# Two-layer masked attention on one core: the reciprocals of layer 1's softmax sums taken later, and its last group counted once

## The chip, the cores and the metric

The kernel runs on one core of a Trainium2 chip. The metric is the device time of one execution in microseconds (us); lower is better. The core has a matmul engine (TensorE, PE), three engines for elementwise work (VectorE, DVE; ScalarE, ACT; GpSimd, POOL) and SyncE (SP), whose queue issues most transfers. Each engine works through its own queue in order and waits on semaphores. PSUM is the memory that PE writes, SBUF the working memory of all engines.

## What is computed

Sixteen graphs of 1,024 nodes with 256 features pass through two layers. Each layer is: layer norm and ReLU, attention over the neighbours that the adjacency allows, an output projection, and a sum with the layer's input. Layer 0 has 4 heads of 64, layer 1 has 8 heads of 32. Cut to what matters:

```python
h = jnp.maximum(_layernorm(x, axis=-1), 0.0)
q, k, v = heads(h @ Wq.T + bq), heads(h @ Wk.T + bk), heads(h @ Wv.T + bv)
scores = jnp.einsum('bhnd,bhmd->bhnm', q, k) / math.sqrt(D)
w = jax.nn.softmax(jnp.where(adjacency == 0, -jnp.inf, scores), axis=-1)
out = jnp.einsum('bhnm,bhmd->bhnd', w, v)
x = x + out.transpose(0, 2, 1, 3).reshape(b, n, e) @ Wo.T + bo
```

Layer 0 has no biases of q, k and v. Everything is float32.

## The kernel before

**Groups and steps.** For one graph and one layer, a group is half of the rows (`qh`, 512 queries) and half of the features (`g`, 128 partitions: two heads in layer 0, four in layer 1). A layer has four groups, in the order (qh 0, g 0), (0, 1), (1, 0), (1, 1); the last has `gr.last` set. A group is worked in steps: 8 in layer 1 (one tile of 128 keys for four heads), 4 in layer 0 (two tiles for two heads). One step is: four score matmuls into PSUM (`scores`, L400); on DVE the mask by a minimum (L416) and on ACT the exponential (L421), each in two halves, which give the tile `p` (`exponentials`); two steps later (`LEAD = 2`) the matmuls of `p` with the values into `po` (`weigh`, L433). The softmax is not shifted by a maximum. It divides at the end, so each group also needs the sums of its `p`.

**The stream.** All steps stand in one list: layer 0 of the next graph, layer 1 of this graph, and so on, so a period is 16 steps of layer 0 and 32 of layer 1. `Stream.run` (L479) records them one by one. Other work is put into a table of due work by `later(i, f)`: at step i, after the masks and exponentials. In an odd step `add_tiles` of layer 0 is recorded before what is due. In even steps with a large piece (`LARGE`: projections and `end_half`) the weighing is left to the next step. What is recorded later stands later in its engine's queue. Each engine follows its queue strictly.

**Sums of layer 1.** For every pair of steps POOL adds the odd tile to the even one (L534). An ordinary group chains its four even tiles by three accumulating transfers (`accumulate`, L520, from POOL's queue, 1 MB each): the first tile into the second at j = 3, the second into the third at j = 7, the third into the fourth three steps after that. Then the fourth is counted once, by matmuls with ones into `pz` (`count`, L301), 8 steps after j = 7 is weighed. The last group of a layer is `brief`: only the first transfer is made, and the second, third and fourth tile are counted one after the other into the same `pz`, all in one step. The last graph's groups (`pairs`, and `hurry` for the very last) count every pair.

**From sums to rows.** `end_group` (L558) sets the steps for what follows, relative to the step i in which the group's last step is weighed:
- `spread`: ACT copies `pz` to `s` (L320), and SP spreads one row per head over the partitions of `sums` (L333, four small transfers);
- `invert`: DVE takes the reciprocal (L341), SP writes it to DRAM (`vd`, L343) and reads it back broadcast (`inv`, L346, four transfers);
- `normalize`: POOL multiplies the group's half of `cat` by `inv` (L352);
- `end_half`, after the second group of a half: the output projection on PE (L381), the sum with the rows on DVE (L386) and, in layer 1, the store from SP (L388).

`inp.test`, seven steps after a layer's last group is weighed, lets DVE check that the sums lie in a range (L247). If they do not, a slower program runs afterwards; in the runs here it does not.

**Beside that.** For a later graph the adjacency is loaded in eight pieces from POOL's queue (L128), each is transposed by a transfer from SP's queue (`flip`, L134) and turned into a mask by ACT (`put`, L143). There is one buffer for a loaded piece, so the next load waits until the transpose is through. `open_x` loads the rows of a later graph (L115) into a buffer that a store has to release, and `half_inputs` and `norms` set the steps of the next layer's projections.

**Positions.** In the following a position is the place of a step in its period, counted from the first step of layer 0 (0 to 15), with layer 1 at 16 to 47; `a` in the code is position 0 and `c` position 16. The groups of layer 1 are weighed to their end at positions 25, 33, 41 and, for the last, 1 of the next period.

Of the kernel before, what the change touches and what calls it, by code (L numbers as in the profile page):

```python
# [82 lines left out]
def fast_program(ctx, tc, a, w, loads, chk):  # L83
# [5 lines left out]
    B, N, E = x.shape  # L89
# [29 lines left out]
    class Mask:  # L119
        def __init__(self, b):  # L120
            self.b, self.src, self.flipped, self.m = b, {}, {}, {}
# [150 lines left out]
    class Group:  # L272


        def __init__(self, inp, mask, qh, g, half):
            self.inp, self.mask, self.qh, self.g, self.half = inp, mask, qh, g, half
            self.layer = inp.layer
            self.D = E // HEADS[self.layer]
            self.per = P // self.D
            self.scale = 1.0 / math.sqrt(self.D)  # L280
            self.n = f"{inp.n}_{qh}_{g}"
            self.n_f = self.per * 512 // P
            self.last = qh == QH - 1 and g == 1

            self.hurry = False

            self.brief, self.pairs = self.last, False

        def steps(self):
            n_j = NT if self.layer else NT // 2  # L290
# [168 lines left out]
    class Stream:  # L459
# [12 lines left out]
        def later(self, i, f, *args):  # L472
            self.due.setdefault(i, []).append((f, args))
# [48 lines left out]
        def count_steps(self, i, st):  # L522


            gr, j = st.gr, st.j
            if gr.hurry and j >= NT - 2:
                if st.last:
                    self.counted(i, gr)
                gr.count(st.p, False, st.last)
            elif j % 2:  # L530
                one = self.steps[i - LEAD - 1].p
                if not (gr.brief or gr.pairs) and j == 7:
                    self.accumulate(gr.two, gr.one)
                nc.gpsimd.tensor_add(one, one, st.p)  # L534
                if gr.pairs:
                    self.later(i + 2, gr.count, one, j == 1, st.last)
                elif j == 1:
                    gr.one = one
                elif j == 3:
                    self.accumulate(one, gr.one)  # L540
                    gr.one = one
                    if gr.brief:
                        self.later(i + 8, gr.count, one, True, False)
                elif gr.brief:
                    self.later(i + (6 if j == 5 else 4), gr.count, one, False, st.last)
                elif j == 5:
                    gr.two = one
                else:
                    self.later(i + 3, self.accumulate, one, gr.two)
                    self.later(i + 8, gr.count, one, True, True)  # L550

        def counted(self, i, gr):

# [4 lines left out]
        def end_group(self, i, gr):  # L558

            if gr.hurry:  # L560
                for f in (gr.spread, gr.finish, gr.inp.test):
                    self.later(i, f)
                return

            if gr.layer == 0:
                self.later(i + 4, gr.count_added)
                at = 4, 6, 8, 11
            else:
                at = (8, 10, 15, 17)
                if gr.pairs:  # L570
                    at = 2, 5, 7, 9
                elif gr.brief:
                    at = 4, 7, 9, 11
            for k, f in zip(at, (gr.spread, gr.invert, gr.normalize)):
                self.later(i + k, f)
            if gr.last:

                k = 7 if gr.layer or gr.inp.b == 0 else 37
                self.later(i + k if gr.inp.b + gr.layer < B - 1 else len(self.steps) + 2, gr.inp.test)
            if gr.g == 1:  # L580
                self.later(i + at[3], gr.end_half)
# [8 lines left out]
    mask, inp = masks[0], inputs[0][0]  # L590
# [74 lines left out]
    later = stream.later  # L665

    def norms(inp, half, *at):

        for i, f in zip(at, (inp.stats, inp.stats, inp.norm, inp.norm)):
            later(i, f, half, (0, 1) if i in (at[0], at[2]) else (2, 3))  # L670
        later(at[3] + 1, inp.add_bias, half)

    def half_inputs(inp, half, *at):

        for i, f in zip(at, (inp.turn, inp.k, inp.q, inp.values)):
            later(i, f, half)
# [5 lines left out]
    for t in range(NT):  # L682
        i = 6 + 2 * t
# [8 lines left out]
    for b in range(B - 1):  # L692
        mine, a, c = inputs[1][b], first[b + 1], second[b]
        if b == 0:

            norms(mine, 0, a + 5, a + 6, a + 8, a + 9)
            half_inputs(mine, 0, a + 11, a + 12, a + 14, a + 14)
            norms(mine, 1, a + 13, a + 14, a + 15, c)
            half_inputs(mine, 1, c + 1, c + 3, c + 6, c + 4)
        else:  # L700
            norms(mine, 0, a - 20, a - 19, a - 16, a - 15)
            half_inputs(mine, 0, a - 13, a, a + 4, a + 8)
            norms(mine, 1, a - 14, a - 10, a - 8, a - 6)
            half_inputs(mine, 1, a - 1, c, c + 6, c + 2)
        for i, u in zip((0, 2, 4, 6, 8, 10, 12, 13), range(NT)):
            later(a + i, masks[b].second, u)
        if b + 2 < B:
            other, mask = inputs[0][b + 2], masks[b + 2]
            later(a + 3, open_x, b + 2, 0)
            later(a + 13, open_x, b + 2, 1)  # L710
            if b == 0:
                norms(other, 0, a + 14, a + 15, c + 2, c + 3)
                half_inputs(other, 0, c + 5, c + 8, c + 16, c + 18)
                norms(other, 1, c + 3, c + 4, c + 6, c + 7)
                half_inputs(other, 1, c + 11, c + 22, c + 26, c + 30)
            else:
                norms(other, 0, a + 10, a + 12, a + 13, a + 15)
                half_inputs(other, 0, c + 1, c + 8, c + 16, c + 18)
                norms(other, 1, c, c + 4, c + 5, c + 6)
                half_inputs(other, 1, c + 9, c + 22, c + 26, c + 30)  # L720
            for i, t in zip((7, 12, 17, 22, 33, 37, 41, 45), range(NT)):
                later(a + i - 5 + (t > 4), mask.load, t)
                later(a + i - 2, mask.flip, t)
                later(a + i, mask.put, t)
        else:
            last, e = inputs[1][b + 1], c + 32
            norms(last, 0, c + 5, c + 6, c + 8, c + 9)
            half_inputs(last, 0, c + 11, c + 14, c + 16, c + 20)
            norms(last, 1, c + 13, c + 14, c + 16, c + 17)
            half_inputs(last, 1, c + 19, c + 24, e + 6, e + 4)  # L730
            for u in range(NT):
                later(c + 8 + 2 * u, masks[b + 1].second, u)
# [158 lines left out]
def kernel(  # L891
# [28 lines left out]
    with ExitStack() as fast, tc.manual_schedule():  # L920
        fast_program(fast, tc, a, w, loads, chk)
# [61 lines left out]
```

## Time and profile before

| | |
|---|---|
| median of 3 runs | 3360.76 us (3353.34 to 3380.53) |
| the profiled execution | 3366.5 us |
| its span, first to last instruction | 3364.7 us |
| granted PE clock | 0.985 |
| accumulating transfers p<-p (L520) | 150, 1024 KB each, median 8.4 us from issue to landing |
| transposes of the adjacency (L134) | 124, 3.0 / 3.3 / 12.8 us to landing (least, median, most) |
| matmuls of the count (L301) | 1,112 records, 172.7 us busy |
| ACT's mask (L143) | 140.6 us busy, 28.1 us idle before it, waiting for transposes |
| POOL's normalizing multiply (L352) | 127, mean 1332 ns |
| median to landing: sums / vd of layer 1 / inv | 1.8 / 2.5 / 2.6 to 2.9 us |

The profile is one execution. Each engine's busy time is the union of its instructions; PE's matmuls are pipelined and their ends are modelled. A matmul in the program leaves two records. In a row of the timeline the first number is the start from the beginning of the span, the second the duration of the merged instructions; the square bracket at the end holds how long the engine was idle before it and what ended that. In the chain of waits each piece is what the end of the kernel hung on at that time.

### The profile page before, as it was taken

The page shows a single profiled execution, that of the slowest core. Times are in us where ns is not written, and L with a number is a line of the kernel's source. Part 1 is how long each engine was busy: PE and PEld are TensorE (multiplying, and loading weights), DVE is VectorE, ACT ScalarE, POOL GpSimd, SP SyncE. Part 2 cuts the span into 40 slices and gives each one's busy share as a digit, 9 for nine tenths or more (in the row PEclk, how much of TensorE's full clock was granted, in tenths as well). Part 3 has the DMA queues.
Part 4 walks back from the last instruction along what each step waited for, and adds up shares of the span by engine and source line. Part 5 has one row for each costly group of instructions (what it writes and reads, how often), then busy time and mean ns, then how long its engine had stood idle before and what let it go on. Part 6 is the DMA issues. An engine that isn't in the chain of part 4 may idle for free.

```text
span 3364.7 us, 44402 instructions
## 1 busy us (share of the span) xinstructions
PE 3267.3 (97%) x16990; PEld 1277.7 (38%) x16990; DVE 2518.0 (75%) x2760; ACT 2181.5 (65%) x2402; POOL 2347.4 (70%) x1244
## 2 busy tenths in 40 slices
PE   8999999999999999999999999999999999999898
PEld 3343333333433333343333433343343333433333
DVE  5776877768767787776877768777687777778876
ACT  6567576665756757667575665757667576674565
POOL 4578586775857758677585776857668586785776
PEclk9999999999999999999999999999999999999899
DMA  7348265472644826447273472736638365380431
GB/s 141 67 76 146 62 120 101 86 145 58 125 92 85 145 64 126 92 88 139 63 140 78 94 144 56 144 77 106 128 64 149 71 109 112 76 154 26 86 79 31
DMA packets 309453, 331.74 MB, mean 99 GB/s; under 512 B 189552, under 2 KB 257392, under 8 KB 290032
## 3 DMA queue, kind: packets, MB, share of 16 engines
q0 software_dynamic: 73824, 224.42, 37.1%
q1 hardware_dynamic: 235408, 104.41, 13.8%
q8 instruction: 135, 2.21, 0.3%
q14 instruction: 86, 0.70, 0.1%
HBM read 119.54 MB, written 17.56 MB: 41 GB/s over the span
## 4 chain that ended last, share of the span: by engine, by line
PE 77%; DMA 7%; ACT 5%; DVE 4%; POOL 3%; issue 2%; SPq 2%; DVEq 0%; ACTq 0%; POOLq 0%
PE ps L400 26%; PE po L433 23%; PE pq L225 11%; PE py L381 7%; PE pv L262 6%; PE pz L301 4%; DVE p L416 3%; DMA sums<-s 3%; DMA p<-p 3%; POOL p L534 3%; ACT p L421 2%; SPq L333 1%; DMA adjT<-adj 1%; ACT mask L143 1%; PE ph L208 1%
## 5 line engine op out<-in xcount | busy, mean ns | idle before, releaser
L421 ACT ACTIVATE p<-p 128x1024 f32<-128x1024 f32 x1536 | 1617.8, 1057 | 938.1 <-DVE p L416 892.4
L416 DVE SCALAR_TENSOR_TENSOR p<-mask,ps 128x1024 f32<-128x1024 fp8e4 x1536 | 1792.0, 1214 | 564.7 <-PE ps L400 547.8
L534 POOL TENSOR_TENSOR p<-p,p 128x2048 f32<-128x2048 f32 x255 | 1190.7, 4672 | 267.0 <-PE po L433 237.5
L400 PE MATMUL ps<-qT,kT 32*128 32x512 f32 (+1 forms) x6144 | 1187.2, 641 | 42.4 <-DVE p L416 40.8
L433 PE MATMUL po<-p,v 128*32 128x512 f32 (+1 forms) x6144 | 1003.0, 608 | 10.9 <-ACT p L421 10.3
L400 PEld LDWEIGHTS ps<-qT,kT 32*128 32x128 f32 (+1 forms) x6144 | 377.2, 186 | 739.0 <-issue 343.6
L446 POOL TENSOR_TENSOR p<-p 128x1024 f32<-128x1024 f32 x128 | 318.7, 2490 | 303.8 <-DVE p L445 298.8
L433 PEld LDWEIGHTS po<-p,v 128*32 128x32 f32 (+1 forms) x6144 | 230.0, 118 | 704.6 <-issue 521.9
L445 POOL TENSOR_TENSOR p<-p 128x1024 f32<-128x1024 f32 x64 | 151.4, 2366 | 263.5 <-DVE vn L341 162.0
L262 PE MATMUL pv<-wv,hT 128*128 128x256 f32 x1024 | 241.6, 390 | 14.5 <-ACT hT L209 14.5
L225 PE MATMUL pq<-hT,wk 128*128 128x512 f32 x512 | 239.9, 612 | 1.5 <-ACT hT L209 1.3
L381 PE MATMUL py<-wo,cat 128*128 128x256 f32 x1008 | 236.6, 388 | 2.3 <-ACT hT L209 1.0
L225 PE MATMUL pq<-hT,wq 128*128 128x512 f32 x512 | 236.6, 605 | 0.1
L262 PEld LDWEIGHTS pv<-wv,hT 128*128 128x128 f32 x1024 | 192.3, 193 | 91.5 <-issue 29.3
L381 PEld LDWEIGHTS py<-wo,cat 128*128 128x128 f32 x1008 | 188.5, 192 | 74.0 <-issue 48.6
L520 POOL DMA_DIRECT2D p<-p x150 | 150.9, 1006 | 40.2 <-POOL p L534 22.2
L352 POOL TENSOR_TENSOR cat<-cat,inv 128x512 f32<-128x512 f32 x127 | 169.2, 1332 | 12.3 <-DMA inv<-vd 8.9
L301 PE MATMUL pz<-p,ones 128*32 128x512 f32 (+1 forms) x1112 | 172.7, 595 | 0.8 <-ACT s L320 0.8
L448 POOL TENSOR_TENSOR p<-p,p 128x1024 f32<-128x1024 f32 x64 | 156.2, 2440 | 5.0
L143 ACT ACTIVATE mask<-adjT,mhalf 128x1024 fp8e4<-128x1024 bf16 x124 | 140.6, 1135 | 28.2 <-DMA adjT<-adj 28.1
L442 DVE TENSOR_TENSOR p<-p 128x1024 f32<-128x1024 f32 x128 | 156.0, 1218 | 0.0
L225 PEld LDWEIGHTS pq<-hT,wk 128*128 128x128 f32 x512 | 93.6, 193 | 146.9 <-issue 102.5
(50 smaller groups left out, 1688.6 us busy)
## 6 DMA issues: line engine op xcount, KB each, us to landing
p<-p POOLq DMA_DIRECT2D x150, 1024.0 KB, 8.4
adj<-in_adj_dram POOLq DMA_DIRECT2D x128, 256.0 KB, 4.1
x<-bo POOLq DMA_DIRECT2D x64, 512.0 KB, 5.9
x<-in_x_dram SPq DMA_DIRECT2D x32, 512.0 KB, 4.4
inv<-vd SPq DMA_DIRECT2D x128, 128.0 KB, 2.9
inv<-vd SPq DMA_DIRECT2D x252, 64.0 KB, 2.6
out_dram<-x SPq DMA_DIRECT2D x31, 512.0 KB, 3.0
sums<-s SPq DMA_DIRECT2D x384, 2.0 KB, 1.8
```

The costliest lines, as they stand in the source:

```text
L143: nc.scalar.activation(self.m[qh][:, :, ts(t % 4, P)], self.flipped.pop(t), AF.Identity, bias=w.mhalf[:, 0:1], saturate=False,)
L225: nc.tensor.matmul(pq[:, m, :], wt[self.layer][:, c, ts(m, P)], self.hT[half][:, c, :], start=(c == 0), stop=(c == 1),)
L262: nc.tensor.matmul(pv[:, i, :], self.hT[half][:, c, ts(i, P)], w.v[self.layer][:, c, :], start=(c == 0), stop=(c == 1),)
L301: nc.tensor.matmul(self.s[r * self.D : (r + 1) * self.D, :], w.ones[:, : self.D], p[:, r, :], start=start, stop=stop,)
L352: nc.gpsimd.tensor_mul(o, o, self.inv)
L381: nc.tensor.matmul(py[:, i, :], self.half.cat[:, c, ts(i, P)], w.o[self.layer][:, c, :], start=(c == 0), stop=(c == 1),)
L400: nc.tensor.matmul(st.ps[i // 2][:, i % 2, :], gr.inp.kT[r * D : (r + 1) * D, gr.g, ts(kt, P)], gr.inp.qT[gr.qh][r * D : (r + 1) * D, gr.g ...
L416: nc.vector.scalar_tensor_tensor(out=half, in0=gr.mask.m[gr.qh][:, kt, :].unsqueeze(1).to_broadcast([P, 2, 512]), scalar=BIG, in1=st.ps[i] ...
L421: nc.scalar.activation(half, half, AF.Exp, scale=gr.scale)
L433: nc.tensor.matmul(gr.o[r * D : (r + 1) * D, :], gr.inp.v[:, kt, h * D : (h + 1) * D], st.p[:, i, :], start=(kt == 0), stop=(kt == NT - 1),)
L446: nc.gpsimd.tensor_add(a, a, b)
L534: nc.gpsimd.tensor_add(one, one, st.p)
```

## The change

```diff
-            self.brief, self.pairs = self.last, False
+            self.brief, self.pairs = self.last and inp.b == B - 2, False
...
                     self.later(i + 3, self.accumulate, one, gr.two)
-                    self.later(i + 8, gr.count, one, True, True)
+                    self.later(i + (6 if gr.last else 8), gr.count, one, True, True)
...
-                at = (8, 10, 15, 17)
+                at = (8, 12, 17, 19) if gr.qh == 0 else (8, 11, 14)
                 if gr.pairs:
                     at = 2, 5, 7, 9
                 elif gr.brief:
                     at = 4, 7, 9, 11
+                elif gr.last:
+                    at = 6, 8, 10, 11
...
-            half_inputs(mine, 0, a - 13, a, a + 4, a + 8)
+            half_inputs(mine, 0, a - 13, a, a + 2, a + 8)
...
-            later(a + 3, open_x, b + 2, 0)
+            later(a + 5, open_x, b + 2, 0)
```

The four numbers of `at` are the steps of `spread`, `invert`, `normalize` and `end_half` after the weighing. In 14 of the 16 graphs the last group of layer 1 is no longer `brief`: its tiles are chained by three transfers, as in the other groups, and the last tile is counted once. In positions of the period the steps go as follows:

| group | count | spread | invert | normalize | end_half |
|---|---|---|---|---|---|
| qh 0, g 0 | 33 | 33 | 35 to 37 | 40 to 42 | |
| qh 0, g 1 | 41 | 41 | 43 to 45 | 0 to 2 | 2 to 4 |
| qh 1, g 0 | 1 | 1 | 3 to 4 | 8 to 7 | |
| qh 1, g 1 (last) | 5 (three) to 7 (one) | 5 to 7 | 8 to 9 | 10 to 11 | 12 |

(One number: unchanged.) The two transfers that are new in the last group are issued at positions 1 and 4. The q projection of layer 1's first half (`half_inputs`) goes from position 4 to 2, and the load of the next rows (`open_x`) from 3 to 5. Nothing is changed in what is computed but the order in which the last group's sums are added.

## The prediction

> **What bounds the kernel now.** I read the page from the top: busy shares, then the chain of work that ended last.
>
> ```profile
> PE 3267.3 (97%) x16990; PEld 1277.7 (38%) x16990; DVE 2518.0 (75%) x2760; ACT 2181.5 (65%) x2402; POOL 2347.4 (70%) x1244
> PE 77%; DMA 7%; ACT 5%; DVE 4%; POOL 3%; issue 2%; SPq 2%; DVEq 0%; ACTq 0%; POOLq 0%
> ```
>
> TensorE (PE) ends the kernel, but a tenth of the chain runs through transfers and queues. The stretches say where. Below are two: a stage of layer 0 and the stage of layer 1 behind it (us, then busy us of PE, PE's weight loads, DVE, ACT, POOL, then granted clock, share of the DMA engines, GB/s):
>
> ```profile
> 1174.00:1257.00 83.00, 83.00 (x375) 32.23 (x376) 66.78 (x76) 45.36 (x51) 47.14 (x26) 1.00 0.24 58
> 1257.00:1380.00 123.00, 119.90 (x690) 46.98 (x688) 89.28 (x97) 91.58 (x101) 100.15 (x53) 0.99 0.73 133
> ```
>
> In layer 0 PE has no gap and the DMA engines are a quarter busy: what PE does less there, it gains, and what it waits there, it loses. In layer 1 PE has gaps, POOL works 81% and the DMA engines 73%: there a removed wait may only uncover another. I count positions in one period of 48 steps: 0 to 15 are layer 0 of one batch, 16 to 47 layer 1 of the batch before; the last groups of the previous layer 1 are finished in 0 to 12. A period takes 204 to 213 us, the first 221 (from its first score matmul to that of the next), and 14 periods hold the changed work.
>
> **The counts.** The chain of waits in layer 0 shows the count of an ordinary group and, at position 5, the three counts of a last group:
>
> ```profile
> 1178.01 0.86 PE pz L301 x8
> ...
> 1200.99 2.71 PE pz L301 x24
> ```
>
> The three become one at position 7: 2.71 - 0.86 = 1.85 us less, 14 times: -26 us, all on PE's path. POOL gets two more accumulating transfers per last group, issued at positions 1 and 4 (about 1.0 us each by the page's L520 row, 28 us in all): POOL is 57% busy in layer 0, so they cost nothing by themselves. The second goes behind L446 of position 3, which ends at 1194.1 in this period, and lands some 8.4 us (the median of p<-p) later, by 1203; the count's turn at position 7 is at 1207.49 - 2.71 + 1.92 + 1.87 = 1208.6. Without those 5 us of cover each us late is one of PE's. The buffer of the last tile is next wanted at position 12, so nothing waits for it.
>
> **The normalising multiply.** This is the step on which I put most weight. In the last group `normalize` moves from position 10 to 11, and `end_half` stays at 12. Positions 11 and 12 of one period, now:
>
> ```profile
> 1022.42 1.28 POOL L352 TENSOR_TENSOR cat<-cat,inv 128x512 f32<-128x512 f32 x1
> 1023.63 1.22 DVE L442 TENSOR_TENSOR p<-p 128x1024 f32<-128x1024 f32 x1
> 1025.02 2.37 POOL L445 TENSOR_TENSOR p<-p 128x1024 f32<-128x1024 f32 x1 [1.32 <-DVE vn L341]
> 1025.22 3.72 PE L381 MATMUL py<-wo,cat 128*128 128x256 f32 x16
> 1027.47 2.69 POOL L446 TENSOR_TENSOR p<-p 128x1024 f32<-128x1024 f32 x1
> ```
>
> Position 11 is odd, so layer 0's `add_tiles` is recorded there ahead of what is due: L445 and L446 enter POOL's queue, and L352 goes behind them. L445 waits for DVE's L442, which ends at 1024.85. So L352 can't begin before 1030.16 and ends at 1030.16 + 1.28 = 1031.4; the output projection that reads it stood ready at 1025.22. PE waits 6.2 us with all that is queued behind it: the scores of position 13, two steps' weighing and a count. The same sum gives 6.2 in thirteen of the 14 places and 6.8 in the last. If DVE came to L442 as early as its scores allow, it would be 0.8 less; if its queue is late by the moved test (below), up to 3 more: 5.4 to 9.4, I take 6.2, since all rows agree: 14 x 6.2 = +87 us. Layer 0 has no gap of PE to pay it back from.
>
> **Four steps behind the copy.** The view of the reciprocal's line:
>
> ```profile
>   DMA sums<-s: 88.4, 28
> ```
>
> All 28 waits are in layer 1 at positions 35 and 43, two per period, 1.2 to 8.4 us. `invert` goes to 37 and 45; two steps' masks are 4.7 us of DVE (2 x 2.35, the L416 pairs there), so nearly all waits as such go. But not all of it is gained. One period with a small first wait (1.77):
>
> ```profile
> 2584.07 0.90 POOL L520 DMA_DIRECT2D p<-p  x1
> 2584.20 1.27 SPq L134 DMA_TRANSPOSE adjT<-adj  x1
> ...
> 2592.95 1.15 ACT L143 ACTIVATE mask<-adjT,mhalf 128x1024 fp8e4<-128x1024 bf16 x1 [6.29 <-DMA adjT<-adj]
> ...
> 2598.41 0.25 DVE L341 RECIPROCAL vn<-sums 128x16 f32<-128x16 f32 x1 [5.84 <-DMA sums<-s]
> ```
>
> The transposed adjacency was issued 0.13 us after an accumulating transfer and took 8.7 us; ACT waited 6.29 for it, the copy of the sums stood behind that on ACT, and DVE's 5.84 is only the end of that chain. The three largest waits (8.4, 7.5, 5.8) are all of this kind. In most other periods it is like this:
>
> ```profile
> 1141.31 1.25 SPq L134 DMA_TRANSPOSE adjT<-adj  x1
> 1141.85 1.28 POOL L352 TENSOR_TENSOR cat<-cat,inv 128x512 f32<-128x512 f32 x1 [1.76 <-DMA inv<-vd]
> 1143.07 0.91 POOL L520 DMA_DIRECT2D p<-p  x1
> ```
>
> Here L352 (position 40) waits and holds the accumulating transfer back until 1.8 us after the transpose, which lands in 3.1 us. The change takes L352 to position 42, behind that transfer: it is then issued about when the one before it lands, 1139.7, some 1.2 us ahead of the transpose. Of the 14 transposes at this place, those with an accumulation issued 0.8 to 0.1 us ahead took 7.9 to 10.8 us, one with it 0.4 behind 6.0, the other ten 3.0 to 3.7. I therefore expect the slow transpose in every period. Counted from the first score matmul of position 30, the transpose is issued at 41 to 42 in every period (its load has just landed), so it lands at about 48.3 instead of 44.1, and ACT, there at 43 to 44, stands some 5 us. Then POOL's next load issue (0.6), L352 (1.3) and L534 (4.6), in this order, free DVE's buffer at 54.8; DVE masks position 45 until 57.2; PE's projection (3.7), scores (1.1), weighing (1.9) and transposes (1.0) follow, and position 47 ends at 57.2 + 0.3 + 7.7 = 65.2; by ACT's queue (mask 1.1, copy 0.6, two norms 1.1, exponentials of 42 to 45 at 2.1: 59.5, then weighing, transposes and what is left of the projection) it can be 66. The 14 periods now have 64.6 to 73.6 there, 67.7 on average. I take 65.7, so 2.0 us gained per period, -28 us. The ends: 4.7 if the transpose lands at 44 (ACT does not stand, some 2.7 less than 65.7), and -1.3 if it takes 10.8 (3.3 more).
>
> The Trainium skill (DMA: Bandwidth & Descriptors, "Issuing engines are not separate DMA queues") states that transfers of all queues run on the same 16 DMA engines and interleave. Read as an even share, it would make the transpose twice 3.1 = 6.2 us, an estimate, and the gain 1.2 us per period larger (-17 us on the sum); the 8.7 of the row speaks for more than sharing.
>
> **What else moves.** The last group's sums are spread at position 7, its `test` stays at 8: DVE's check of the sums (L247) now waits for those transfers, behind it on DVE the next step's masks, and PE behind these. The copy comes at ACT about 4 us before, the four sums land in 1.7 to 3.4 us after issue: 0 to 1 us, hidden as the 4.5 us that these checks take now at the same place are. SyncE's queue at positions 4 and 5 becomes one chain: four inverses, store of the rows, load of x, transpose, beside the new accumulation. Now the transpose there has 14 us before ACT needs it; I expect 1 to 3 us left, and take +4 us in all, bounds 0 and +45 (3 us per period). The q projection and the output projection exchange positions 2 and 4: the same matmuls, nothing. The `normalize` that goes from 0 to 2 now stands behind POOL's last L534 (to 1181.9 in the period from 1170) and ends at 1183.2; its projection's turn at 4 is 1191.9: nothing. The reciprocal that goes from 3 to 4 waits for nothing now and comes later.
>
> **Sum.** -26 + 87 - 28 + 4 = +37 us. The profiled execution took 3366.5 us (span 3364.7), 5.7 above the median, 3360.8; on the median: 3398 us, 1.1% slower.
>
> **Rivals.**
> 1. More is lost in layer 1 and at SyncE: slow transposes of 10.8 us and the x chain late. -26 + 87 + 18 (14 x 1.3) = +79, with no gain from the waits at all: 3440. For it: DMA share 0.73 there already. Against: the normalising multiply no longer waits in front of POOL's additions.
> 2. The waits go and the transposes stay at 3.1 us, because the accumulation starts late enough: -26 + 87 - 66 = -5: 3356. It decides at an issue 0.7 us behind the transpose.
> 3. Faster: the projection at 12 does not wait, because L352 is through before 1025.2. It needs DVE's L442 6.2 us earlier; its scores allow 0.8. -26 - 28 = -54: 3307. The change would then do just what it says.
> 4. Four steps do not suffice, the waits stay: against it, they are at most 8.4 us and the long ones have another cause.
>
> **Numbers.** Forecast 0.60, rival 1 0.20, rival 2 0.12, rival 3 0.07, rival 4 0.01. About 1% (34 us) is what a measurement of this kernel can tell from no change, and the forecast lies just beyond it: its own range is 3370 to 3425, slightly more than half of it beyond 3394. Slower: 0.32 + 0.20 = 0.52; faster: 0.07 and the low end of rival 2, 0.09; the rest 0.39. Range 3348 to 3446: rival 2 a little below its middle, rival 1 a little beyond it.
>
> **What would show it.** After: a gap of 6 us before the output projection L381 released by POOL L352, 14 times, in the chain too; pz x888 instead of 1112 (14 x 16 records fewer); L341's idle time near zero; L143's idle time grown from 28 to 50 us or more; L520 x178. It is wrong if L381 shows no wait, or if L143's stays near 28 with layer 1 shorter by 4 us.

## The result and the profile after

| | before | after |
|---|---|---|
| median (4 runs each, side by side) | 3367.1 us | 3443.2 us (3440.74 to 3446.12) |
| ratio to before | | 1.024 [1.021, 1.028] |
| profiled execution / its span | 3366.5 / 3364.7 us | 3440.7 / 3439.0 us |
| granted PE clock | 0.985 | 0.979 |

The kernel is 2.4% slower by the recorded ratio (the quotient of the two medians alone is 1.023). The forecast was 1.1% slower (+37 us on the profiled execution); it became +74.3 us in the span. The busy shares and the chain of work that ended last, from the page after:

```profile
PE 3264.3 (95%) x16766; PEld 1288.3 (37%) x16766; DVE 2557.7 (74%) x2760; ACT 2169.1 (63%) x2402; POOL 2371.8 (69%) x1272
PE 70%; DVE 10%; DMA 6%; POOL 5%; issue 4%; ACT 4%; SPq 1%; ACTq 0%; DVEq 0%; POOLq 0%
```

PE has 224 instructions fewer (14 x 16) and is nevertheless busy 3264.3 us, only 3.0 less. A group whose number of instructions is unchanged says why (columns: busy us, mean ns of one; then the idle time before it and what ended it). From the groups after, with ACT's mask:

```profile
L381 PE MATMUL py<-wo,cat 128*128 128x256 f32 x1008 | 272.1, 427 | 84.2 <-POOL cat L352 81.8
...
L143 ACT ACTIVATE mask<-adjT,mhalf 128x1024 fp8e4<-128x1024 bf16 x124 | 140.9, 1137 | 100.6 <-DMA adjT<-adj 100.6
```

and the projection's group before:

```profile
L381 PE MATMUL py<-wo,cat 128*128 128x256 f32 x1008 | 236.6, 388 | 2.3 <-ACT hT L209 1.0
```

The output projection now waits 81.8 us for the normalising multiply, which was predicted; and the same 1,008 records cost 35.5 us more of PE's busy time, which was not. One place of the 14, in the timeline after:

```profile
1030.82 1.22 DVE L442 TENSOR_TENSOR p<-p 128x1024 f32<-128x1024 f32 x1
...
1032.21 2.35 POOL L445 TENSOR_TENSOR p<-p 128x1024 f32<-128x1024 f32 x1 [2.56 <-DVE vn L341]
1032.25 0.70 PE L381 MATMUL py<-wo,cat 128*128 128x256 f32 x2
...
1034.64 2.67 POOL L446 TENSOR_TENSOR p<-p 128x1024 f32<-128x1024 f32 x1
...
1037.28 1.26 POOL L352 TENSOR_TENSOR cat<-cat,inv 128x512 f32<-128x512 f32 x1
...
1038.59 5.69 PE L381 MATMUL py<-wo,cat 128*128 128x256 f32 x14 [5.63 <-POOL cat L352]
```

Read down POOL: L445 begins only after DVE's L442, which ends at 1032.04 (the bracket names the reciprocal that DVE does just then; it is L442 that L445 needs done), L446 follows, and L352, which was through at 1023.70 before, comes third. PE does the two records that need only the other half of `cat`, then stands 5.63 us. But look at the last row: 14 records take 5.69 us, 0.41 us each, where 16 took 3.72 us before. The windows after give the reason (columns as in the prediction, the granted clock third from the end):

```profile
1032.30:1038.50 6.20, 0.65 (x4) 0.25 (x2) 3.94 (x7) 3.15 (x3) 6.12 (x3) 0.85 0.01 1
1038.50:1042.00 3.50, 3.41 (x8) 2.79 (x9) 0.00 (x0) 0.00 (x0) 2.38 (x6) 0.50 0.21 75
1042.00:1045.00 3.00, 3.00 (x11) 1.98 (x12) 0.69 (x1) 0.00 (x0) 0.00 (x0) 0.75 0.55 87
1045.00:1055.00 10.00, 10.00 (x46) 3.13 (x44) 8.12 (x8) 5.98 (x8) 4.53 (x2) 1.00 0.35 105
```

After the gap the granted clock is 0.50, and 1.00 again only about 5 us after PE is back at work. The wait is paid twice: as idle time, and as slow matmuls behind it. (Experiments 2 and 3 test that the clock is the reason.)

**Where the 74.3 us lie**, as differences of the time between the first score matmuls of positions, summed over 14 periods:

| positions | predicted | measured |
|---|---|---|
| 4 to 8, the counts | -26 | -23.8 (1.70 each) |
| 12, the projection | +87 | +119.6 (8.5 each) |
| 30 to 48, layer 1, with the first period | -28 | -21.3 |
| everything else | +4 | -0.2 |

**Layer 1.** The reciprocal L341 has no idle time left (88.4 us before). What took its place is the transposed adjacency, in a period like the second one shown in the prediction:

```profile
1156.13 0.91 POOL L520 DMA_DIRECT2D p<-p  x1 [1.40 <-PE pz L301]
...
1158.01 2.08 SPq L134 DMA_TRANSPOSE adjT<-adj  x1
...
1164.79 1.15 ACT L143 ACTIVATE mask<-adjT,mhalf 128x1024 fp8e4<-128x1024 bf16 x1 [6.23 <-DMA adjT<-adj]
...
1165.32 0.60 POOL L128 DMA_DIRECT2D adj<-in_adj_dram  x1 [3.72 <-DMA adjT<-adj]
...
1165.93 1.29 POOL L352 TENSOR_TENSOR cat<-cat,inv 128x512 f32<-128x512 f32 x1
...
1167.17 4.54 POOL L534 TENSOR_TENSOR p<-p,p 128x2048 f32<-128x2048 f32 x1
...
1171.75 2.35 DVE L416 SCALAR_TENSOR_TENSOR p<-mask,ps 128x1024 f32<-128x1024 fp8e4 x2 [4.49 <-POOL p L534]
```

The accumulating transfer now goes out ahead of the transpose; the transpose lands late; ACT waits 6.23 us for it and POOL 3.72, and POOL's addition frees DVE's buffer so late that DVE waits 4.49 at position 45. The table of waits sums that. Before:

```profile
PE ps L400 <- DVE p L416: 40.8, 26, 7.2
...
PE po L433 <- ACT p L421: 10.3, 3, 5.2
```

After:

```profile
PE po L433 <- ACT p L421: 33.2, 14, 3.2
...
PE ps L400 <- DVE p L416: 13.3, 6, 7.2
```

(The columns are the sum in us, the times and the longest.) PE used to wait mostly for DVE's masks; now it waits for ACT's exponentials, 14 times, 3.2 us at most. So of 88.4 us of waits some 21 came out as time. Part of these 21 may be the clock: in the 14 periods that have the transposes, layer 1 ran at a granted clock of 0.50 for 64.9 us before and for 20.5 after. At half speed the difference of 44.4 us can be worth up to 22 us (an estimate from these two figures); no run separates it from the waits.

### The profile page after: what moved, and what is told of

The parts are those of the page before. It is cut to its first block, busy times and chain, and to the rows that moved or that the text cites. A ratio compares the mean times of both kernels' runs of the same rounds, so it can differ in the third digit from the quotient of the medians.

```text
span 3439.0 us, 44053 instructions
## 1 busy us (share of the span) xinstructions
PE 3264.3 (95%) x16766; PEld 1288.3 (37%) x16766; DVE 2557.7 (74%) x2760; ACT 2169.1 (63%) x2402; POOL 2371.8 (69%) x1272
## 3 DMA queue, kind: packets, MB, share of 16 engines
q0 software_dynamic: 77856, 253.78, 40.8%
## 4 chain that ended last, share of the span: by engine, by line
PE 70%; DVE 10%; DMA 6%; POOL 5%; issue 4%; ACT 4%; SPq 1%; ACTq 0%; DVEq 0%; POOLq 0%
PE ps L400 22%; PE po L433 20%; PE pq L225 11%; PE py L381 7%; DVE p L416 5%; PE pv L262 5%; DMA adjT<-adj 3%; POOL p L534 3%; PE pz L301 3%; ACT p L421 2%; DVE chk L247 1%; DVE p L442 1%; PE ph L208 1%; DVE mask L151 1%; POOL p L445 1%
## 5 line engine op out<-in xcount | busy, mean ns | idle before, releaser
L400 PE MATMUL ps<-qT,kT 32*128 32x512 f32 (+1 forms) x6144 | 1162.8, 635 | 14.8 <-DVE p L416 13.3
L433 PE MATMUL po<-p,v 128*32 128x512 f32 (+1 forms) x6144 | 1015.1, 604 | 34.2 <-ACT p L421 33.2
L446 POOL TENSOR_TENSOR p<-p 128x1024 f32<-128x1024 f32 x128 | 316.9, 2476 | 389.4 <-DVE p L445 384.4
L381 PE MATMUL py<-wo,cat 128*128 128x256 f32 x1008 | 272.1, 427 | 84.2 <-POOL cat L352 81.8
L445 POOL TENSOR_TENSOR p<-p 128x1024 f32<-128x1024 f32 x64 | 151.4, 2366 | 247.5 <-DVE p L442 165.6
L381 PEld LDWEIGHTS py<-wo,cat 128*128 128x128 f32 x1008 | 210.1, 215 | 169.2 <-POOL cat L352 87.7
L520 POOL DMA_DIRECT2D p<-p x178 | 175.2, 984 | 112.1 <-DMA p<-p 62.3
L143 ACT ACTIVATE mask<-adjT,mhalf 128x1024 fp8e4<-128x1024 bf16 x124 | 140.9, 1137 | 100.6 <-DMA adjT<-adj 100.6
L386 DVE TENSOR_TENSOR x<-py,x 128x1024 f32<-128x1024 f32 x63 | 77.2, 1225 | 149.1 <-PE py L381 148.2
L352 POOL TENSOR_TENSOR cat<-cat,inv 128x512 f32<-128x512 f32 x127 | 168.9, 1330 | 9.9 <-DMA inv<-vd 7.3
L151 DVE TENSOR_SCALAR mask<-mask 128x1024 fp8e4<-128x1024 fp8e4 x128 | 170.1, 1329 | 0.0
L442 DVE TENSOR_TENSOR p<-p 128x1024 f32<-128x1024 f32 x128 | 156.0, 1219 | 0.0
```

What stands on the lines that cost most here:

```text
L151: nc.vector.tensor_scalar(m, m, -0.5, 0.5, op0=ALU.not_equal, op1=ALU.subtract, saturate=False)
L381: nc.tensor.matmul(py[:, i, :], self.half.cat[:, c, ts(i, P)], w.o[self.layer][:, c, :], start=(c == 0), stop=(c == 1),)
L400: nc.tensor.matmul(st.ps[i // 2][:, i % 2, :], gr.inp.kT[r * D : (r + 1) * D, gr.g, ts(kt, P)], gr.inp.qT[gr.qh][r * D : (r + 1) * D, gr.g ...
L433: nc.tensor.matmul(gr.o[r * D : (r + 1) * D, :], gr.inp.v[:, kt, h * D : (h + 1) * D], st.p[:, i, :], start=(kt == 0), stop=(kt == NT - 1),)
L442: nc.vector.tensor_add(a, a, b)
L445: engine.tensor_add(b, two.p[:, 0:2, :], two.p[:, 2:4, :])
```

## The experiments

All ratios are to the kernel before, run on the same chip beside them (medians 3365.4 us for experiments 1, 2, 4 and 5, 3370.4 us for the others). Its single executions lie between 3352.6 and 3387.0 us, so a difference of a few us between two spans, each of one profiled execution, says little; sums over the 14 places in layer 0 say more (that of the counts is -23.7 to -24.0 in all eight kernels that have the change). Theory: the terms of the prediction's sum are right in kind and independent; the missing 33 us are PE's clock after the gap. Rivals stand in each expectation.

**1. The multiply back at position 10.**

```diff
-                    at = 6, 8, 10, 11
+                    at = 6, 8, 9, 11
```

> The changed kernel with the last group's normalize at position 10 instead of 11 (reciprocal still at 9), so that POOL's multiply L352 stands ahead of L445 and L446. Theory (the output projection at 12 loses 8.5 us per period, 6 by waiting for L352 and 2.5 by the halved clock that follows the idle time): both go, 14 x 8.5 = 119 us less than the changed kernel, near 3324; L381's idle time after POOL L352 falls from 82 us to under 10. Rival (the slow projection has its own cause, transfers or ports beside it): only the wait goes, 14 x 6 = 84 less, near 3359. Rival (the inverse, written and read back after the reciprocal at 9, lands too late for position 10): POOL waits for inv, L381 for L352, and 30 us or more stay.

3324.56 us, ratio 0.987 [0.984, 0.990]. Position 12 is 0.06 us per period longer than before, against 8.5 in the changed kernel; the counts' -1.70 stay. POOL does the multiply ahead of layer 0's additions, and PE finds it done:

```profile
1005.20 1.28 POOL L352 TENSOR_TENSOR cat<-cat,inv 128x512 f32<-128x512 f32 x1
...
1007.69 3.72 PE L381 MATMUL py<-wo,cat 128*128 128x256 f32 x16
1007.73 2.37 POOL L445 TENSOR_TENSOR p<-p 128x1024 f32<-128x1024 f32 x1 [1.25 <-DVE vn L341]
```

One step of one multiply is worth 3.6%, and turns slower into faster.

**2. PE kept busy while it waits.** The multiply stays at 11. Fourteen matmuls whose result is overwritten stand ahead of the projection (the line numbers behind them are 5 higher: L386 is the projection).

```diff
+            if self.last and self.layer and inp.b < B - 2:
+                for k in range(14):
+                    nc.tensor.matmul(
+                        py[:, k % 4, :], w.ident, w.o[1][:, 0, :], start=True, stop=True
+                    )
```

> The changed kernel with 14 extra matmuls (28 records, about 6.0 us) into the projection's own PSUM tile ahead of the last group's projection; they are overwritten by it. PE then works through the wait for L352. Theory (clock halved by the idle time): granted clock stays 1.0 around the projection, its matmuls stand 0.21 us apart instead of 0.43, 14 x 2.5 = 35 us less than the changed kernel, near 3408. Rival (the projection is slow from transfers or ports): still 0.43 us apart, no gain, near 3443 or up to 10 more.

3414.11 us, ratio 1.014 [1.011, 1.017]: more work on PE, and 29 us less than the changed kernel. From the timeline:

```profile
1024.14 6.31 PE L381 MATMUL py<-wo,ident 128*128 128x256 f32 x28
1030.29 3.62 PE L386 MATMUL py<-wo,cat 128*128 128x256 f32 x16
```

In twelve of the 14 places the extra matmuls fill the wait to its end (in two, 0.92 us of idle time remain), and the projection behind them takes 3.62 us, for 3.72 before. Position 12 is 87.7 us longer than before in 14 periods; in the twelve places the extra matmuls themselves set that length. The other 119.6 - 87.7 = 31.9 us are the clock. The changed kernel's own rows say nearly the same: its 14 projections last 33.2 us longer behind the gap than 14 times the 3.29 us that the same 14 records take at full clock (experiment 3).

**3. Only half of the wait filled.** As 2, with 7 extra matmuls, so that PE is idle for what remains.

```diff
-                for k in range(14):
+                for k in range(7):
```

> The changed kernel with 7 extra matmuls (overwritten, not used) instead of 14 ahead of the last group's output projection: they fill about 3 us of the 6, PE is idle for the other 3. The wait for L352 stays, so position 12 is at least 6.0 us longer than before. Theory A (the clock is halved only by an idle stretch longer than about 3 us): clock 1.0 in most periods, position 12 longer by 6.0 to 6.7 us, 1.014 of before (1.011 to 1.018), mean granted clock 0.99. Rival B (any stretch of idle time of this length halves it, so what counts is that PE was idle at all): position 12 longer by about 8.5 us, ratio 1.021 to 1.027, mean clock 0.98.

3433.98 us, ratio 1.019 [1.016, 1.023], clock 0.987, which is between the two. The periods separate. In six the gap was 3.8 to 3.9 us, in seven 2.6, in the last 2.0. One of each, from the timeline:

```profile
615.89 6.21 PE L386 MATMUL py<-wo,cat 128*128 128x256 f32 x14 [3.92 <-POOL cat L352]
...
1036.70 3.29 PE L386 MATMUL py<-wo,cat 128*128 128x256 f32 x14 [2.63 <-POOL cat L352]
```

The same 14 records take 6.21 us behind the one gap and 3.29 behind the other; the granted clock there, from the windows:

```profile
616.00:619.50 3.50, 3.50 (x9) 2.78 (x10) 0.00 (x0) 0.00 (x0) 2.29 (x5) 0.50 0.24 75
...
1036.70:1040.00 3.30, 3.30 (x16) 2.66 (x16) 0.00 (x0) 0.00 (x0) 2.36 (x5) 1.00 0.29 79
```

All six long gaps cost 1.5 to 3.0 us behind them. Of the seven gaps of 2.6 us, four cost nothing and three 1.4 to 1.7 us. The long gaps agree with theory and rival alike; of the short ones four agree with theory A and three with rival B. What sets the two kinds of short gap apart can be read in the clock's rows of the trace. In all ten traces here the granted clock is 1.00 or 0.50, and it changes only at multiples of 3.41 us from its first change. Cut at these steps, a harmless short gap (1034.07 to 1036.70) and a costly one (1666.12 to 1668.74):

```profile
1031.45:1034.86 3.41, 2.62 (x13) 1.96 (x11) 2.90 (x6) 3.08 (x3) 3.33 (x2) 1.00 0.00 0
1034.86:1038.28 3.42, 1.58 (x7) 1.42 (x8) 0.00 (x0) 0.00 (x0) 3.18 (x5) 1.00 0.05 17
...
1666.33:1669.74 3.41, 1.00 (x5) 0.90 (x6) 0.17 (x1) 0.31 (x1) 3.24 (x4) 1.00 0.00 0
1669.74:1673.15 3.41, 3.41 (x10) 2.65 (x9) 0.00 (x0) 0.00 (x0) 1.48 (x4) 0.50 0.47 96
```

The first gap is divided by a step into 0.8 and 1.8 us of idle time; the second has 2.4 us between two steps, and the stretch to the next step is at 0.50. All seven short gaps go this way: the three costly ones have 2.1 to 2.7 us between two steps, the four others at most 1.84. In the ten traces, after the first 90 us, every gap that began at full clock and had 2.0 us or more between two steps is followed by 0.50; the longest one that is not, 3.33 us in experiment 6, is divided into 1.87 and 1.46. This was read from the traces afterwards; no run moved a gap against the steps.

**4. The later reciprocals alone.** The kernel before with the changes to the ordinary groups and to `half_inputs` and `open_x`; the last group stays `brief`.

```diff
-                at = (8, 10, 15, 17)
+                at = (8, 12, 17, 19) if gr.qh == 0 else (8, 11, 14)
```

> The kernel before with only the later reciprocals of layer 1's ordinary groups (with their normalize and end_half, the q projection at 2 and the load of rows at 5); the last group is counted in three as before. Theory (the transposes at position 39 become slow in every period, as they follow an accumulating transfer): L341 waits for nothing, L143 waits 80 us or more, and of the 88 us of waits only some 20 are gained: 0.6% faster than before, ratio 0.994, 0.991 to 0.998. Rival (waits of DVE are worth what they last): 88 us, ratio 0.974. Rival (the chain of inverses, store, load and transpose at positions 4 and 5 costs): ratio over 1.0.

3350.53 us, ratio 0.995 [0.993, 0.997], span -14.9. The reciprocal's 88.4 us of waiting are gone, a naive 2.6%; a sixth of that is gained. The wait that came instead, from the table of ACT's waits:

```profile
ACT mask L143 <- DMA adjT<-adj: 91.7, 16, 7.8
```

All 14 transposes of position 39 took 6.5 to 9.4 us.

**5. The first group's multiply back at position 40**, everything else as in the changed kernel.

```diff
-                at = (8, 12, 17, 19) if gr.qh == 0 else (8, 11, 14)
+                at = (8, 12, 17 if gr.g else 15, 19) if gr.qh == 0 else (8, 11, 14)
```

> The changed kernel with normalize of the group (qh 0, g 0) back at position 40, so that L352 holds the accumulating transfer back until the inverse has landed. Theory (the order of that transfer and the transpose decides): the transpose of position 39 is slow less often, L143's wait falls from 100 us to under 40, layer 1 is 2 to 3 us shorter per period, 28 to 42 us less than the changed kernel, near 3408; the stall of L381 stays at 82 us. Rival (POOL, held by the inverse, frees DVE's buffers later): L143's wait falls but the time does not, 3435 to 3450.

3417.25 us, ratio 1.014 [1.010, 1.017]. Twelve of the 14 transposes take 3.0 to 3.1 us again, two 4.9 and 5.0. The table of waits, ACT's row:

```profile
ACT mask L143 <- DMA adjT<-adj: 48.7, 31, 5.7
```

and POOL's:

```profile
POOL cat L352 <- DMA inv<-vd: 48.5, 19, 3.7
```

The multiply's wait for its inverse, 48.5 us of POOL's time, holds the accumulating transfer back, and that is worth 18 us of span (3439.0 to 3421.3; 26 us of the medians, as the profiled execution is the slowest of the four). Of ACT's wait 48.7 us remain where less than 40 was expected, and the time is 9 us above the expected 3408: the direction is right, the size was set too high. One period is 8.3 us longer at positions 30 to 36, nearly the whole difference. There a transpose was issued at 1951.82 and an accumulating transfer 0.76 us behind it; they took 17.6 and 19.2 us (the median of these transfers is 8.0), and ACT and POOL waited for them. Why these two were so slow is open.

**6. The chained last group alone**, multiply at 10, nothing of the later reciprocals.

```diff
-            self.brief, self.pairs = self.last, False
+            self.brief, self.pairs = self.last and inp.b == B - 2, False
...
-                    self.later(i + 8, gr.count, one, True, True)
+                    self.later(i + (6 if gr.last else 8), gr.count, one, True, True)
...
+                elif gr.last:
+                    at = 6, 8, 9, 11
```

> The kernel before with the chained last group, counted once, and with its normalising multiply left at position 10 (steps 6, 8, 9, 11); the later reciprocals and the moved projections and load are left out. Theory (terms add): 1.70 us per period from the three counts made one, 14 times, -24 us, and nothing else: 0.993 of before (0.990 to 0.996), the output projection L381 does not wait for L352, the reciprocal's waits in layer 1 stay at about 88 us. Rival 1: the two new accumulating transfers and the new chain at SyncE cost something in layer 0 that the later reciprocals hid: 0.996 to 1.003. Rival 2: the counts' place is paid back in layer 1 (PE arrives earlier and waits there for the same transfers): layer 1 longer by 10 us or more, ratio over 0.996.

3341.97 us, ratio 0.993 [0.990, 0.996]; positions 4 to 8 give -24.0 us, the rest of layer 0 moves by 0.0, layer 1 by -0.5 (its periods move by -7.7 to +6.1 and nearly cancel). The reciprocal's waits are 100.4 us, for some 88 expected. The two new accumulating transfers cost nothing in layer 0. The span is 25.0 shorter; with the 14.9 of experiment 4 that makes 39.9, and experiment 1, which has both, has 41.7. By the medians it is 28.4 + 14.8 = 43.2 for 40.8. So the terms add, as far as such differences can tell.

**7. Both multiplies moved back.** Experiments 1 and 5 in one kernel.

> The changed kernel with both multiplies put back ahead of what they now stand behind: the last group's at position 10 and that of the first group of layer 1 at position 40. Theory: 3324.6 (the first alone) - 26 (what the second alone took off the changed kernel) = 3298 us, ratio 0.980 (0.976 to 0.984); transposes of position 39 take about 3 us in twelve periods of 14. Rival: the two are not independent; with PE 8.5 us earlier in the period, layer 1 waits for its transfers instead, and the ratio stays at 0.984 to 0.988.

3296.28 us, ratio 0.979 [0.975, 0.982], span 3293.6: 2.1% faster than before and 147 us faster than the change. The period of the timeline to set beside the one after:

```profile
1115.57 1.26 SPq L134 DMA_TRANSPOSE adjT<-adj  x1
1115.84 1.28 POOL L352 TENSOR_TENSOR cat<-cat,inv 128x512 f32<-128x512 f32 x1 [3.14 <-DMA inv<-vd]
1117.06 0.92 POOL L520 DMA_DIRECT2D p<-p  x1
...
1118.71 1.15 ACT L143 ACTIVATE mask<-adjT,mhalf 128x1024 fp8e4<-128x1024 bf16 x1 [2.19 <-DMA adjT<-adj]
```

The transpose is out 1.5 us ahead of the accumulating transfer and lands in about 3 us. POOL's 3.14 us of waiting cost nothing that shows.

**8. The projection later instead of the multiply earlier.** The multiply stays at 11, the projection goes to 14; the next rows' load and layer norm, which need its buffer, go two steps later too.

```diff
-                    at = 6, 8, 10, 11
+                    at = 6, 8, 10, 13
...
-            later(a + 13, open_x, b + 2, 1)
+            later(a + 15, open_x, b + 2, 1)
...
-                norms(other, 1, c, c + 4, c + 5, c + 6)
+                norms(other, 1, c + 2, c + 4, c + 5, c + 6)
```

> The changed kernel with its multiply left at position 11, but the projection that reads it moved from position 12 to 14 (steps 6, 8, 10, 13); the load of the next rows goes from 13 to 15 and the first layer norm of that half from 16 to 18, since they need the projection's buffer. PE reaches the projection some 8 us later. Theory (the multiply behind POOL's additions harms only by what PE finds in front of it): no wait of L381 for L352, no halved clock in layer 0, -24 - 21 = -45 us against before, 0.987 (0.983 to 0.991). Rival: the later projection delays the store, the load of the next rows and the layer norm behind them; a wait at positions 16 to 20 of 2 to 4 us per period takes 28 to 56 us back: 0.995 to 1.004.

3328.75 us, ratio 0.988 [0.985, 0.992]. From the timeline:

```profile
1011.00 1.30 POOL L352 TENSOR_TENSOR cat<-cat,inv 128x512 f32<-128x512 f32 x1
...
1014.04 3.72 PE L381 MATMUL py<-wo,cat 128*128 128x256 f32 x16
```

The multiply still stands behind L446, but PE comes for it 1.7 us after its end, and nothing waits. Positions 12 to 16 together are 0.9 us longer than before. So the multiply's place in POOL's queue harms only through what PE finds in front of it.

## Why the prediction was wrong, point by point

**The step that failed is the price of the normalising multiply's stall: "PE waits 6.2 us with all that is queued behind it", "14 x 6.2 = +87 us".** About the wait itself its place, its releaser and its count of 14 were right, and its size nearly: without the 33.2 us that the projections lose to the clock, position 12 is 86.4 us longer, for 87. That this agrees to the microsecond is partly luck: ten places have 5.9 us, where PE does two records in the meantime, three have 6.9 to 7.6 with DVE late, and the last, for which 6.8 was forecast, has 5.3. What the step left out is that PE does not come out of the gap at its old speed: the granted clock is 0.50 afterwards, and the 14 records that follow take 5.69 us instead of 3.29 (experiment 3). That makes 8.5 us per period, +119.6. The bounds given for this term, 5.4 to 9.4, held it, but only for another reason (DVE being late). The profile of before already had the clock as a column, 1.00 where PE had no gap, and no gap of 6 us in layer 0 to read the price from. In layer 1 it had the price, in a period of which the prediction quotes an earlier stretch (from 1141 us on):

```profile
1151.92 1.13 PE L400 MATMUL ps<-qT,kT 32*128 32x512 f32 x4
1154.82 2.07 PE L400 MATMUL ps<-qT,kT 32*128 32x512 f32 x4 [1.77 <-DVE p L416]
```

```profile
1154.60:1161.40 6.80, 6.58 (x22) 1.82 (x23) 4.15 (x5) 5.27 (x5) 6.50 (x4) 0.50 1.14 191
```

Behind a gap of only 1.77 us four score records take 2.07 us where four took 1.13, and the granted clock is 0.50 for 6.8 us.

The Trainium skill (TensorE: Matmul & The Clock Gate, "Part 1: The HAM clock gate (the "warmup" mystery)") says that PE's clock is either full or half, is halved after an idle window of about 3.4 us, and needs about as long at work to come back. The halving to 0.50 behind the changed kernel's gaps of 5.0 to 6.9 us, and behind all those of 3.8 to 3.9, agrees; three gaps of only 2.6 us were followed by slow matmuls as well, so a gap shorter than the window is not safe here. Applied to the prediction, the page gives an estimate of 3.4/2 = 1.7 us per gap, 24 us in all, against 31.9 measured; it would have put the sum at +61.

**The counts**: -23.8 for -26. The difference of two merged pieces of the chain (1.85) was 0.15 too much; the group's busy time, 172.7 to 148.7 us, gives 1.71 each. The cover claimed for the two new transfers held (experiment 6).

**Four steps behind the copy**: the mechanism was right in each link. No wait is left at L341, and all 14 transposes at position 39 are slow: 5.9 to 8.7 us, 7.5 on average. The 8.7 is that of the quoted row; the sum itself has the transpose issued at 41 and landed at 48.3, which is 7.3. Measured, it is issued at 41.6 and lands at 49.1 on average. The skill's interleaving, read as an even share, made 6.2 of it. The landings do not look like a share: in the changed kernel each of the 14 transposes lands 0.8 to 1.4 us after the accumulating transfer issued ahead of it, which itself takes its usual 7.5 to 9.0 us; the transpose takes what is left of that transfer. The row's 8.7 was one of these with a lead of 0.1 us; a lead of about 1 us takes as much off. The end mark of layer 1 was put at 65.7 us and came to 66.2 from 67.7, a gain of 1.5 us per period for 2.0: -21.3 for -28. How much of it is the waits and how much the clock of layer 1 (64.9 us at 0.50 before, 20.5 after) is open; the sum had no term for the clock here either.

**What else moves**: +4 was taken, -0.2 measured. The check of the sums and SyncE's chain at positions 4 and 5 showed no loss.

**The sum**: of the 37.3 us missed, 32.6 come from position 12, 6.7 from layer 1, 2.2 from the counts, and -4.2 from the rest.

**The rivals.** Rival 1 named a time near the result, 3440, for a wrong reason: it had layer 1 18 us slower, and layer 1 is 21 faster. Rival 2 needed transposes of 3.1 us, which the changed kernel has nowhere at this place; experiments 5 and 7 have them, and layer 1 is then 37 and 50 us shorter, not 66. Rival 3, no stall, is experiment 1: its -54 came out as -41.7, because layer 1 gives 19 and not 28, and the counts 24. Rival 4 falls: the waits of L341 are gone. The range's upper end, 3446, held the result by 3 us; the forecast's own range, 3370 to 3425, did not.

**The signs named ahead** all came: the gap before L381 14 times, `pz` x888, `p<-p` x178, L341 without idle time, L143's idle time over 50 (100.6). Not named: the mean duration of L381, 388 to 427 ns, which shows the missing term in one row.

## What to carry to other kernels

Price a new stall of the matmul engine as its length plus what runs slowly behind it: here about 6 us of waiting cost 8.5, and filling the wait with matmuls that nobody reads gained 29 us. When an operation moves by one step on an engine that works in order, list what is recorded between the old place and the new one; moving the producer ahead of it or the consumer behind it cures the stall alike. And a wait on one engine may be what spaces two transfers: take it away, and look at which transfer now meets which.

## What the runs showed of the hardware that was not expected

- In front of the projection PE's clock falls to 0.50 behind gaps of 3.8 us and more, each time in these runs, and behind three of seven gaps of 2.6 us; in layer 1 a gap of 1.77 us was followed by 0.50 as well. The cost was 1.4 to 3.0 us per gap whatever its length, so a longer gap is not the dearer one in this part.
- The clock changes only at steps 3.41 us apart, and a gap is followed by 0.50 when enough of it lies between two steps: always with 2.0 us or more, in four gaps of 2.6 us with at most 1.84 not.
- A transpose that takes 3.0 to 3.1 us by itself ends about when an accumulating transfer of 1 MB ends that was issued 0.8 to 3.0 us ahead of it. In the changed kernel and in experiments 4 and 8 that is so for 42 transposes of 42, which land 0.8 to 1.7 us after the transfer (one 2.7) and so take 5.9 to 9.4. Issued 1.5 to 2.2 us ahead of the transfer (experiments 5 and 7), 24 of 28 take 3.0 to 3.1 and four 4.5 to 5.0. Issued only 0.76 us ahead, one elsewhere in experiment 5 took 17.6. Whether every transfer waits like this behind an accumulating one, or only a transpose, was not tried.
